# Two graph attention layers: the last attention's products issued as two column halves of the array

## The chip, the cores and the metric

The kernel runs on one core of a Trainium2 chip, in one launch. The metric is the device time of that core in microseconds (us); lower is better. Before the change the median of three runs is 3426.05 us, the lowest 3424.98 and the highest 3427.45.

A core has a matrix engine (TensorE), VectorE, ScalarE, GpSimd and DMA queues, here mostly issued from SyncE. TensorE computes `out = lhsT.T @ rhs`: the operand `lhsT` is loaded into the array first (an LDWEIGHTS record in the trace), then `rhs` streams past it (a MATMUL record) and the result is written to PSUM. The columns of `lhsT` become the partitions of the result.

## The reference

64 graphs of 256 nodes with 512 features each, all in fp32, go through two layers. Each layer normalises its input, applies a ReLU, runs attention over the edges of the graph and adds the result to its input. The second layer is the one that matters here. Cut to it:

```python
# x: (64, 256, 512), adj: (64, 256, 256); H = 8 heads of k = 64 features
h  = jnp.maximum(_layernorm(x, axis=-1), 0.0)
xp = jnp.einsum('bnd,do->bno', h, W_proj)
xh = xp.reshape(B, N, H, k).transpose(0, 2, 1, 3)
a_src = jnp.einsum('bhnk,hk->bhn', xh, W_att[:, :k])
a_dst = jnp.einsum('bhnk,hk->bhn', xh, W_att[:, k:])
scores = leaky_relu(a_src[:, :, :, None] + a_dst[:, :, None, :] + b_att[None, :, None, None], 0.2)
scores = jnp.where((adj > 0)[:, None, :, :], scores, -1e30)
att = softmax(scores, axis=-1)
out = relu(einsum('bhij,bhjk->bhik', att, xh))        # the products that are changed
x   = x + out.transpose(0, 2, 1, 3).reshape(B, N, H * k)
```

The first layer has two attentions of its own, with 4 heads of 256 features and with 1 head of 512 features.

## The kernel before

A graph passes through three attentions, numbered 1, 2 and 3. In each, VectorE and ScalarE build the unnormalised edge weights `e` of a head (256 x 256, source nodes on the partitions in two tiles `s`, target nodes along the row); TensorE multiplies them with the projected features `xl`, to which a column of ones is appended, so that the last column of the result is the sum of the weights; VectorE divides by it. The work of three successive graphs is interleaved by one hand-written order.

The large projections go through one helper, which holds most of TensorE's other work. Its products have 256 to 264 moving columns (`put` adds up partial sums of a Strassen-like scheme; seven such products stand for eight):

```python
P = 128                                                                # line 18
class Product:
    def product(self, to, i, first, last):
        for c in range(self.nk):
            self.nc.tensor.matmul(to[:, :self.n], self.lhs[:, i, c, :], self.rhs[:, i, c, :],      # line 54
                                  start=(first and c == 0), stop=(last and c == self.nk - 1),
                                  skip_group_check=True)
    def kept(self, name):
        s = self.work.tile([P, 268], F32, name=name)
        self.nc.scalar.activation(s[:, :self.n], self.sum[:, :self.n], AF.Copy)                    # line 60
        return s
    # ... p1 to p7: the products in their order ...
```

Buffers in PSUM, and the transposes and edge weights:

```python
T, G, K3, H3, Q = 2, 4, 64, 8, 256
ps_sum = tile_pool(name="ps_sum", bufs=2, space=PSUM)
ps_mm  = tile_pool(name="ps_mm", bufs=4, space=PSUM)
ps_tr  = tile_pool(name="ps_tr", bufs=2, space=PSUM)
xl3 = const.tile([P, T, H3, K3 + 1], F32, name="xl3")      # the last column is 1.0
# ...
nc.tensor.transpose(pt[:, k, t * P:(t + 1) * P], h(t, c + k), ident)                               # line 193
# ...
def weigh(dst, bc, xw, yw, mask, op):
    wy = work.tile([P, T, P], F32, name="wy", bufs=3)
    nc.scalar.activation(wy, bc, AF.Copy, scale=yw)                                                # line 273
    nc.vector.scalar_tensor_tensor(dst, wy.rearrange("p t q -> p (t q)"), xw, mask, ALU.max, op)   # line 274
```

The third attention, whose product is changed:

```python
def edges3(self, h):
    e = self.e[3, h] = work.tile([P, T, N], F32, name="e", bufs=8)
    for s in range(T):
        weigh(e[:, s, :], self.bc3[h], self.ex3[:, 0, h, s:s + 1], self.ex3[:, 1, h, s:s + 1],
              self.cap[:, s, :], ALU.min)

def gat3(self, a, t):                     # a: four heads of the eight, t: 128 nodes of the 256
    pm = self.pm = ps_mm.tile([P, 512], F32, name="pm")
    pv = pm[:, :G * (K3 + 1)].rearrange("p (h k) -> p h k", h=G)
    for h in range(G):
        for s in range(T):
            nc.tensor.matmul(pv[:, h, :], self.e[3, a * G + h][:, s, t * P:(t + 1) * P],           # line 445
                             xl3[:, s, a * G + h, :], start=(s == 0), stop=(s == T - 1))

def out3(self, a, t):
    pv = self.pm[:, :G * (K3 + 1)].rearrange("p (h k) -> p h k", h=G)
    r = small.tile([P, G, 1], F32, name="r3")
    nc.vector.reciprocal(r, pv[:, :, K3:])                                                         # line 451
    o = work.tile([P, G, K3], F32, name="o", bufs=4)
    nc.vector.scalar_tensor_tensor(o, pv[:, :, :K3], 0.0, r.to_broadcast([P, G, K3]), ALU.max, ALU.mult)
    # ... GpSimd adds o to x2 (line 455) ...
```

The products of attentions 1 and 2 (`gat1`, line 348, and `gat2`, line 399) have the same form, with 256 or 257 moving columns. The order in which the items are issued, cut to the places of gat3; `0` is the current graph, `-1` and `-2` are the two before it:

```python
order = """
    -1 exp2, -2 edges3 0, 0 m1a p2, ... -2 edges3 5,
    -2 gat3 0 0, -2 out3 0 0, 0 m1b p6, -1 edges2, -2 edges3 6, 0 m1b p5, -2 gat3 0 1, -2 out3 0 1, -2 edges3 7,
    0 m1b p7, 0 m1b c22, -1 gat2 0, ... -1 gat2 1, ... 0 gat1 0 0, 0 out1 0 0, -2 gat3 1 0,
    -2 out3 1 0, 0 cap3, -1 stats3 1, 0 gat1 0 1, -1 norm3, 0 out1 0 1, -2 gat3 1 1, 0 elu1 0 0, -2 out3 1 1, -2 store,
    0 gat1 1 0, ...
"""
```

Right at the end a product with 2 weight columns and 1 moving column folds a check over all partitions (line 601):

```python
nc.tensor.matmul(pf[:2, 0, 0:1], top[:, 2:4], ones, start=True, stop=True)                         # line 601
```

Of the kernel before, what the change touches and what calls it, by code (L numbers as in the profile page):

```python
# [17 lines left out]
P = 128  # L18
# [79 lines left out]
def short_path(ctx, tc, flags, x, adj, w1, att_src1, att_dst1, b1, w2, att_src2, att_dst2, b2, w_proj, w_att,  # L98
               b_att, out):

    nc = tc.nc
# [6 lines left out]
    T = N // P  # L108
    DC = D // P
    HC = HF // P  # L110
    G = 4
# [43 lines left out]
    xl3 = const.tile([P, T, H3, K3 + 1], F32, name="xl3")  # L155
# [120 lines left out]
    class Graph:  # L276
# [163 lines left out]
        def gat3(self, a, t):  # L440
            pm = self.pm = ps_mm.tile([P, 512], F32, name="pm")
            pv = pm[:, :G * (K3 + 1)].rearrange("p (h k) -> p h k", h=G)
            for h in range(G):
                for s in range(T):
                    nc.tensor.matmul(pv[:, h, :], self.e[3, a * G + h][:, s, t * P:(t + 1) * P],  # L445
                                     xl3[:, s, a * G + h, :], start=(s == 0), stop=(s == T - 1))

        def out3(self, a, t):
            pv = self.pm[:, :G * (K3 + 1)].rearrange("p (h k) -> p h k", h=G)
# [7 lines left out]
        def range(self):  # L457
            nc.vector.tensor_reduce(ends[:, 0, self.b:self.b + 1], self.exs, AX.X, ALU.max)
            nc.vector.tensor_reduce(ends[:, 1, self.b:self.b + 1], self.exs, AX.X, ALU.min)
# [408 lines left out]
```

## Time and profile before

The profiled execution spans 3421.9 us.

| engine | busy us | share of the span | instructions |
|---|---|---|---|
| TensorE, products (PE) | 3326.7 | 97% | 17668 |
| TensorE, weight loads (PEld) | 2899.3 | 85% | 17668 |
| VectorE (DVE) | 2492.3 | 73% | 6447 |
| ScalarE (ACT) | 1876.7 | 55% | 4481 |
| GpSimd (POOL) | 1231.4 | 36% | 1369 |

The page numbers its parts: busy times; the span in 40 slices, with busy tenths of each engine and the clock granted to TensorE; DMA queues; the chain of work that ended last, as shares of the span by engine and by line; and the costliest groups of instructions, with count, busy time, mean length in ns, and the idle time ahead of them with what ended it. "L445" is line 445 of the kernel. In the groups and in the timeline `out<-in` are the program's tiles; PEld is a weight load and PE a product. Products are pipelined, so that one record overlaps with the next: what one really costs is the step from one start to the next, not its length.

### The profile page before, as it was taken

Reading aid. Unit: us, or ns where it says so; the run is one execution under the profiler, and the core shown is the slowest. Engines: PE = TensorE matmul, PEld = TensorE weight load, DVE = VectorE, ACT = ScalarE, POOL = GpSimd, SP = SyncE. Lnnn points to the kernel's source line nnn. Section 1 sums busy time; section 2 is a strip of 40 time slices with the busy share of each in tenths; the row PEclk is TensorE's granted clock in tenths of the full one; section 3 lists DMA queues with packets and bytes.
Section 4 is the critical chain, followed back from the end, with each engine's and each line's share of the span. In section 5 each row is a group of like instructions: output and inputs, shape, how many; then the busy total and the mean of one; then the engine's idle time right before and its main releaser. Section 6 shows DMA issues by size and latency. Waiting matters only on the chain.

```text
span 3421.9 us, 51905 instructions
## 1 busy us (share of the span) xinstructions
PE 3326.7 (97%) x17668; PEld 2899.3 (85%) x17668; DVE 2492.3 (73%) x6447; ACT 1876.7 (55%) x4481; POOL 1231.4 (36%) x1369
## 2 busy tenths in 40 slices
PE   4899999999999999999999999999999999999997
PEld 3688888888888888888888888888888888888886
DVE  7577777777777777777777777777777777777773
ACT  2355555555555555555565565565565565555553
POOL 1333433333433433433433433433433434334332
PEclk8999999999999999999999999999999999999997
DMA  4223323323223233323323323323223233232331
GB/s 134 58 85 82 82 85 81 83 82 85 83 80 86 81 81 83 85 78 81 90 75 82 92 75 82 90 76 83 86 80 83 81 86 81 80 87 78 84 78 40
DMA packets 354316, 280.87 MB, mean 82 GB/s; under 512 B 159616, under 2 KB 254848, under 8 KB 354048
## 3 DMA queue, kind: packets, MB, share of 16 engines
q1 hardware_dynamic: 352480, 275.40, 29.7%
q8 instruction: 144, 2.36, 0.3%
q10 hardware_dynamic: 1568, 2.10, 0.2%
q14 instruction: 124, 1.02, 0.1%
HBM read 201.07 MB, written 67.96 MB: 79 GB/s over the span
## 4 chain that ended last, share of the span: by engine, by line
PE 88%; ACT 5%; DMA 3%; DVE 2%; issue 1%; POOL 0%; SPq 0%; ACTq 0%; DVEq 0%
PE sum L54 30%; PE pm L54 21%; PE pm L445 13%; PE pm L348 13%; PE pm L399 6%; PE pt L193 5%; ACT wy L273 3%; DMA kept<-exs 1%; DMA bc<-kept 1%; ACT u L60 1%; ACT s L60 0%; DVE wy L492 0%; DMA w1a_sb<-in_L_gnn_W_dram 0%; DVE e L274 0%; POOL o L553 0%
## 5 line engine op out<-in xcount | busy, mean ns | idle before, releaser
L273 ACT ACTIVATE wy<-bc,exs 128x256 f32<-128x256 f32 x1664 | 768.9, 520 | 194.5 <-DMA bc<-kept 79.2
L455 POOL TENSOR_TENSOR x<-x,o 128x256 f32<-128x256 f32 x256 | 197.7, 772 | 1446.0 <-DVE o L453 1446.0
L274 DVE SCALAR_TENSOR_TENSOR e<-wy,exs,cap 128x256 f32<-128x256 f32 x1024 | 486.4, 511 | 141.0 <-ACT wy L273 133.3
L445 PEld LDWEIGHTS pm<-xl,e 128*128 128x128 f32 x4096 | 505.4, 195 | 26.5 <-issue 9.8
L348 PE MATMUL pm<-xl,e 128*128 128x257 f32 x2048 | 496.6, 385 | 9.9 <-DVE e L274 6.5
L445 PE MATMUL pm<-xl,e 128*128 128x65 f32 x4096 | 494.5, 275 | 11.3 <-DVE e L274 11.3
L54 PE MATMUL sum<-w_sb,h1s 128*128 128x257 f32 x2048 | 493.7, 383 | 0.7 <-ACT u L60 0.7
L54 PEld LDWEIGHTS sum<-w_sb,h1s 128*128 128x128 f32 x2048 | 379.9, 190 | 73.6 <-issue 21.8
L246 DVE TENSOR_TENSOR xl<-pm,u 128x256 f32<-128x256 f32 (+2 forms) x512 | 214.8, 419 | 310.0 <-PE pm L54 249.8
L348 PEld LDWEIGHTS pm<-xl,e 128*128 128x128 f32 x2048 | 375.2, 191 | 59.2 <-DVE e L274 8.4
L60 ACT ACTIVATE u<-sum 128x260 f32<-128x260 f32 (+3 forms) x512 | 196.5, 384 | 356.7 <-PE sum L54 350.7
L54 PE MATMUL pm<-w_sb,h1s 128*128 128x257 f32 x1536 | 365.0, 379 | 0.0
L54 PEld LDWEIGHTS pm<-w_sb,h1s 128*128 128x128 f32 x1536 | 290.9, 189 | 43.9
L54 PE MATMUL sum<-w1a_sb,hs 128*128 128x260 f32 x1024 | 274.7, 391 | 36.0 <-DVE hs L206 28.8
L274 DVE SCALAR_TENSOR_TENSOR e<-wy,exs,mask 128x256 f32<-128x256 f32 x640 | 274.7, 476 | 46.9 <-ACT wy L273 46.9
L212 POOL TENSOR_TENSOR hs<-hs 128x256 f32<-128x256 f32 x128 | 93.6, 731 | 543.1 <-DVE hs L206 324.6
L54 PE MATMUL sum<-wp_sb,hs 128*128 128x264 f32 x1024 | 277.3, 393 | 1.2 <-ACT u L60 1.1
L54 PE MATMUL sum<-w1b_sb,hs 128*128 128x256 f32 x1024 | 271.1, 387 | 1.0 <-ACT u L60 1.0
L54 PEld LDWEIGHTS sum<-w1a_sb,hs 128*128 128x128 f32 x1024 | 188.4, 190 | 89.2 <-ACT u L60 32.1
L358 DVE SCALAR_TENSOR_TENSOR z<-pm,r,b_sb 128x256 f32<-128x256 f32 x512 | 247.7, 484 | 18.1
L361 ACT ACTIVATE ez<-z 128x512 f32<-128x512 f32 x256 | 160.4, 627 | 164.9 <-DVE z L358 164.7
L399 PE MATMUL pm<-xl,e 128*128 128x257 f32 (+1 forms) x1024 | 243.8, 381 | 0.8 <-DVE e L274 0.7
(92 smaller groups left out, 5284.7 us busy)
## 6 DMA issues: line engine op xcount, KB each, us to landing
bc<-kept SPq DMA_DIRECT2D x384, 256.0 KB, 3.8
xs<-in_x_dram SPq DMA_DIRECT2D x64, 512.0 KB, 3.9
kept_h<-h SPq DMA_DIRECT2D x64, 512.0 KB, 3.2
h<-kept_h SPq DMA_DIRECT2D x64, 512.0 KB, 3.6
out_dram<-x SPq DMA_DIRECT2D x64, 512.0 KB, 2.8
ad<-in_adj_dram SPq DMA_DIRECT2D x64, 256.0 KB, 4.2
bc<-kept SPq DMA_DIRECT2D x64, 128.0 KB, 4.2
w_sb<-in_L_gnn_W_dram SPq DMA_DIRECT2D x4, 512.0 KB, 9.2
```

The source lines that it names most:

```text
L54: self.nc.tensor.matmul(to[:, :self.n], self.lhs[:, i, c, :], self.rhs[:, i, c, :], start=(first and c == 0), stop=(last and c == self.nk ...
L60: self.nc.scalar.activation(s[:, :self.n], self.sum[:, :self.n], AF.Copy)
L193: nc.tensor.transpose(pt[:, k, t * P:(t + 1) * P], h(t, c + k), ident)
L246: nc.vector.tensor_tensor(dst, pm, add, ALU.add)
L273: nc.scalar.activation(wy, bc, AF.Copy, scale=yw)
L274: nc.vector.scalar_tensor_tensor(dst, wy.rearrange("p t q -> p (t q)"), xw, mask, ALU.max, op)
L348: nc.tensor.matmul(pm[:, :Q + 1], self.e[1, h][:, s, t * P:(t + 1) * P], xl1[:, s, h, L1:], start=(s == 0), stop=(s == T - 1))
L358: nc.vector.scalar_tensor_tensor(z[:, sl], pm[:, :Q], r, b1_sb[:, sl], ALU.mult, ALU.add)
L361: nc.scalar.activation(ez, z[:, 2 * g * F1:2 * (g + 1) * F1], AF.Relu, scale=-1.0)
L399: nc.tensor.matmul(pm[:, :n], self.e[2][:, s, t * P:(t + 1) * P], xl2[:, s, half, L2:L2 + n], start=(s == 0), stop=(s == T - 1))
L445: nc.tensor.matmul(pv[:, h, :], self.e[3, a * G + h][:, s, t * P:(t + 1) * P], xl3[:, s, a * G + h, :], start=(s == 0), stop=(s == T - 1))
L455: nc.gpsimd.tensor_tensor(to, to, o.rearrange("p h k -> p (h k)"), ALU.add)
```

## The change

`gat3` multiplies 128 x 128 edge weights with 128 x 65 features. The change issues each such product as two: the first takes the edge weights of 64 target nodes and writes the upper 64 partitions of the result, the second takes the other 64 nodes and writes the lower 64 partitions. Each has 64 weight columns and lies on its own half of the array's columns. The values computed, the tiles and the order are the same. It is meant to let the two halves of the array, each with its own weights, work at the same time, since a product with 65 moving columns keeps the array occupied with weight loads more than with streaming.

```diff
@@ -440,10 +440,12 @@
         def gat3(self, a, t):
             pm = self.pm = ps_mm.tile([P, 512], F32, name="pm")
             pv = pm[:, :G * (K3 + 1)].rearrange("p (h k) -> p h k", h=G)
+
             for h in range(G):
                 for s in range(T):
-                    nc.tensor.matmul(pv[:, h, :], self.e[3, a * G + h][:, s, t * P:(t + 1) * P],
-                                     xl3[:, s, a * G + h, :], start=(s == 0), stop=(s == T - 1))
+                    for q in range(0, P, 64):
+                        nc.tensor.matmul(pv[q:q + 64, h, :], self.e[3, a * G + h][:, s, t * P + q:t * P + q + 64],
+                                         xl3[:, s, a * G + h, :], start=(s == 0), stop=(s == T - 1))
```

## Prediction

> **What bounds the kernel now.** I read the busy times first, then the 40 slices, then the chain of work that ended last:
>
> ```profile
> PE 3326.7 (97%) x17668; PEld 2899.3 (85%) x17668; DVE 2492.3 (73%) x6447; ACT 1876.7 (55%) x4481; POOL 1231.4 (36%) x1369
> ...
> PE   4899999999999999999999999999999999999997
> ...
> PEclk8999999999999999999999999999999999999997
> ...
> PE 88%; ACT 5%; DMA 3%; DVE 2%; issue 1%; POOL 0%; SPq 0%; ACTq 0%; DVEq 0%
> PE sum L54 30%; PE pm L54 21%; PE pm L445 13%; PE pm L348 13%; PE pm L399 6%; PE pt L193 5%; ACT wy L273 3%; DMA kept<-exs 1%; DMA bc<-kept 1%; ACT u L60 1%; ACT s L60 0%; DVE wy L492 0%; DMA w1a_sb<-in_L_gnn_W_dram 0%; DVE e L274 0%; POOL
> ```
>
> TensorE is the bound from the third slice to the last, at full clock, with VectorE next at 73%. The line that the change touches, L445, holds 13% of the chain: 0.13 x 3422 = 445 us. Whatever it gains or loses goes almost straight into the time. The table of busy time by stretch, over three graphs' worth of the middle (1480 to 1636 us), shows how little slack TensorE has and how much the others have:
>
> ```profile
> 1480.00:1636.00 156.00, 155.65 (x839) 136.10 (x838) 115.50 (x296) 89.09 (x214) 58.41 (x65) 1.00 0.31 82
> ```
>
> (columns: length, PE, PEld, DVE, ACT, POOL, clock, DMA share, GB/s.) A graph costs 52 us, of which TensorE is idle 0.1 us.
>
> A busy TensorE may stream or load weights, so I took L445 apart. In the groups it stands twice, as loads and as products; in the timeline I looked at one call of gat3, weight loads first and then products:
>
> ```profile
> L445 PEld LDWEIGHTS pm<-xl,e 128*128 128x128 f32 x4096 | 505.4, 195 | 26.5 <-issue 9.8
> L445 PE MATMUL pm<-xl,e 128*128 128x65 f32 x4096 | 494.5, 275 | 11.3 <-DVE e L274 11.3
> ```
>
> ```profile
> 1506.88 0.19 PEld L54 LDWEIGHTS pm<-w1a_sb,hs 128*128 128x128 f32 x1
> 1507.10 1.97 PEld L445 LDWEIGHTS pm<-xl,e 128*128 128x128 f32 x16
> ```
>
> ```profile
> 1507.32 1.90 PE L445 MATMUL pm<-xl,e 128*128 128x65 f32 x16
> 1509.05 0.43 PE L54 MATMUL sum<-w1b_sb,hs 128*128 128x256 f32 x1
> ```
>
> The program asks for 64 graphs x 4 calls x 4 heads x 2 = 2048 products, and the trace has 4096 of each kind: every fp32 product is two records. Sixteen records take 1.97 us from the first load. The first load lies 0.22 us early, under the product before it, and the last is 0.19 long, so the 14 steps between take (1.97 - 0.22 - 0.19) / 14 = **0.111 us each**. What fills the 0.111? A line's own answer gives shortest, median and longest record:
>
> ```profile
> L445 PEld LDWEIGHTS pm<-xl,e x4096: 186/192/333, 165.9 to 3412.3; 128*128 128x128 f32 x196
> L445 PE MATMUL pm<-xl,e x4096: 220/275/444, 166.1 to 3412.4; 128*128 128x65 f32 x196
> ```
>
> ```profile
> L601 PEld LDWEIGHTS pt<-ones,top x2: 80/82/83, 3414.7 to 3414.7; 128*2 128x2 f32 x2
> L601 PE MATMUL pt<-ones,top x2: 163/164/165, 3414.7 to 3414.7; 128*2 128x1 f32 x2
> ```
>
> L601 is a tiny product near the end, with 2 weight columns and 1 moving column. Against it a load of 128 columns lasts 192 - 82 = 110 ns longer, 0.87 ns a column: a fixed 80 ns that overlaps with the neighbours, and 110 ns that don't. A product of 65 columns lasts at its shortest 220 - 164 = 56 ns longer than one of 1. So one step of 111 ns is **one weight load**; the streaming, 56 ns, lies under the next load. The usual product of 275 ns is the short one plus 55 ns in which it waits for its weights. On L54, with 256 to 264 moving columns, it is the other way round: loads hide under streaming.
>
> **What the Trainium skill says.** "TensorE: Matmul & The Clock Gate", section "LDWEIGHTS (loading the stationary operand)", has the load's time grow with the number of columns alone, columns / 1.2 ns. That is 107 ns for 128 columns; this trace agrees with 111 per step, and L601 confirms the growth. "FP8 and Floating Point Precision", section "TensorE Precision Notes", says that true FP32 is four passes through the array; two records a product, each 56 ns for 65 columns, fit that. "TensorEngine Tiling (Array Packing)", section "Key Properties", bears on the change itself: tiles of the array may load weights and multiply in parallel, but changing the tiling mode drains TensorE. The first page's "Measured speedup vs the span model" reports 2.38x for three column tiles with 512 moving columns, which shows products side by side, not loads. No run here has column tiles yet, so neither statement is seen in this trace.
>
> **The change part by part.** L445's 4096 records of 128 weight columns become 8192 of 64 columns each; the moving operand, 65 columns, is read once for each half. VectorE's, ScalarE's and GpSimd's work, the transfers and the PSUM tile stay as they are.
>
> (a) One load: 64 of 128 columns, 110 / 2 = 55 ns, say 58 with the step's small fixed part; in the trace its record should last 82 + 62 x 0.87 = 136 ns. The streaming stays 56 ns and still fits under a load of its size.
>
> (b) Two halves in place of one record. If the two tiles' loads run at once, an old step of 111 ns becomes 58, 53 ns less; over 4096 steps that is -217 us. Issue doesn't forbid it: L601's two products start 26 ns apart, each with its load, and 58 ns has to hold two such pairs. If all loads share one way in, 2 x 58 = 116, 5 more than now: 4096 x 5 = +20 us.
>
> (c) Mode changes. Each of the 256 calls stands alone between products of 128 columns (L54, L348, L399), so it is entered and left once, 512 changes. What one costs I estimate from the records: a product lasts 164 ns beyond its streaming (L601), and behind a drain the next weights, now loaded ahead, would follow only after that, with some 50 ns more until the first result streams. I take 0.2 us a change, 0.4 a call: 256 x 0.4 = +102 us.
>
> (d) Passing it on. In the stretch shown, 0.35 us of 156 are waits of TensorE, and VectorE has 115.5 of 156. A gain of (217 - 102) / 64 = 1.8 us a graph leaves VectorE far from being the bound. But when gat3 gets shorter, some products behind it (those waiting for a copy on L60 or for edge weights on L274) come earlier than their input: I take a tenth off. (217 - 102) x 0.9 = 104 us, 3426 - 104 = **3322, say 3320 us**.
>
> **Rivals.**
> 1. *Loads side by side, no drain to speak of.* -217 x 0.9 = -195: about 3230. For it: the page states that tiles work independently. Against it: the same page states the drain.
> 2. *Loads one after another.* In the call shown two loads of 128 columns never come closer than 0.11 us, so today one load is taken in at a time; if it stays so, +20 from (b) and from 0 to +102 from (c): 3445 to 3550. Here the change only moves the wait from one long load to two short ones.
> 3. *Nothing overlaps within a tile.* If a load of 64 columns can't be taken ahead of the running product of the same column tile, and the tiles also take turns, each half costs 58 + 56 = 114 ns and a step 228: 4096 x 117 = +479 us, about 3900. Against it: in the present mode loads do overlap with products on the same rows and columns. For it: no trace here shows what fp32 makes of the column mode. Overlap in part (tiles side by side, load and product of one tile in turn) gives 114 a step, like rival 2.
> 4. *VectorE or ScalarE becomes the bound.* Even rival 1 takes 3.1 of 52 us per graph, against VectorE's 38.5: it doesn't happen as a sum, at most as single waits.
>
> **Range and chances.** Loads side by side get 52% (30% with a drain near my estimate, 3310 to 3345; 22% with little of it, about 3230 to 3260). Loads in turn get 27%, half near 3445, half up to 3550. The rest, 21%, is the lack of overlap of rival 3, anywhere from 3550 to 3900. So low is 3225 and high 3560, with most of the miss above. Faster by over 2% (under 3357.5) 0.50, within 2% 0.18, slower (over 3494.6) 0.32.
>
> **What would show it.** In the profile after: L445 with 8192 loads of 128x64 at about 136 ns median, right for (a). In the timeline of one call, 32 loads within about 0.95 us for side by side, 1.85 us for in turn, 3.6 for rival 3. Around a call, the start of the first product after L54 and the start of the first L54 product after the call: 0.2 us later than 0.22 and 0.11 us for the drain, or not. The slices must keep PE at 9, the clock at 9; the waits of "PE sum" on "ACT u L60", 4.6 us now, growing to tens of us would show that step (d) was too small. The prediction is wrong if loads of the two tiles don't overlap, or if a change of mode costs more than 0.4 us, at which point the gain of a call (16 x 53 ns = 0.85 us) is used up.

## The result and the profile after

The median is 3385.75 us (3385.23 to 3385.99) against 3425.52 us of the kernel before on the same chip: ratio **0.988**, 95% interval 0.987 to 0.990, 40 us less. The prediction was 3320 us, 106 us less. The direction was right; the gain is 0.38 of the one forecast.

First the busy times of the page after, then the table of busy time by stretch over three graphs in the middle (length, PE, PEld, DVE, ACT, POOL, clock, DMA share, GB/s):

```profile
PE 3230.2 (95%) x21764; PEld 2659.8 (79%) x21764; DVE 2503.5 (74%) x6447; ACT 1868.1 (55%) x4481; POOL 1245.1 (37%) x1369
```

```profile
1480.00:1632.00 152.00, 149.05 (x1017) 122.98 (x1016) 114.29 (x291) 87.67 (x210) 57.87 (x63) 1.00 0.30 82
```

TensorE no longer fills the stretch: 2.95 us of 152 are idle, where 0.35 of 156 were before. That is 1 us a graph which the array had saved and then stood still for. (The chain that ended last breaks off after 1% of the span in this page, so it isn't read.)

Now the changed line, L447 after the edit. Its shortest, median and longest record:

```profile
L447 PEld LDWEIGHTS pm<-xl,e x8192: 132/138/232, 167.0 to 3373.5; 128*64 128x64 f32 x200
L447 PE MATMUL pm<-xl,e x8192: 220/222/370, 167.0 to 3373.6; 128*64 128x65 f32 x200
```

A load of 64 columns lasts 138 ns, against 192 for 128. A product's median is 222, the same as its shortest, against 275: it no longer waits 55 ns for its weights. In the timeline, one call of gat3 between two calls of gat1 (start, length, engine, line, tiles, shapes, records, and in brackets idle time with its releaser), before:

```profile
1519.76 0.81 PE L348 MATMUL pm<-xl,e 128*128 128x257 f32 x3
1520.41 1.90 PE L445 MATMUL pm<-xl,e 128*128 128x65 f32 x16
1522.14 1.95 PE L348 MATMUL pm<-xl,e 128*128 128x257 f32 x8
```

and after:

```profile
1506.23 1.03 PE L348 MATMUL pm<-xl,e 128*128 128x257 f32 x4
1507.21 1.15 PE L447 MATMUL pm<-xl,e 128*64 128x65 f32 x32
1508.30 1.13 PE L348 MATMUL pm<-xl,e 128*128 128x257 f32 x4
1509.78 0.46 PE L348 MATMUL pm<-xl,e 128*128 128x257 f32 x1 [0.35 <-DVE r L356]
```

From the call's first start to the next line's first it took 1522.14 - 1520.41 = 1.73 us; now 1508.30 - 1507.21 = 1.09 us, with twice the records. But gat1, which ran its 8 records in one go, now stops after four: its fifth waits until VectorE's reciprocal on L356 has given back a buffer of `pm`. The waits of the whole span show two pairs of entries, each for weight loads and for products, that the kernel before doesn't have at this size (total us, times, longest; a load and its product wait at the same time, so the two don't add up):

```profile
PEld pt L193 <- ACT h L186: 56.8, 128, 2.9
...
PEld pm L348 <- PE pm L348: 46.2, 64, 1.0
...
PE pt L193 <- ACT h L186: 28.3, 66, 2.7
PE pm L348 <- DVE r L356: 24.8, 64, 2.5
```

Before, the transposes on L193 waited 4.9 and 3.9 us for h (L186), and the two entries on `pm` stood at 1.3 and 3.4 us. Each of these waits comes once or twice for each of the 64 graphs.

The change of mode (from the whole array to two column halves, and back) shows at both ends of a call. Before, the first load of a call started 0.22 us ahead of its product, under the product before it (1507.10 and 1507.32 in the lines of the prediction). Now the loads of the same call of gat3, and those of gat1 behind it, start only with their products (1507.21 and 1508.30):

```profile
1507.19 1.03 PEld L447 LDWEIGHTS pm<-xl,e 128*64 128x64 f32 x32 [0.33 <-PE pm L348]
1508.29 0.73 PEld L348 LDWEIGHTS pm<-xl,e 128*128 128x128 f32 x4
```

To see where a graph loses what, I set the starts of all TensorE records of both traces side by side, in program order, over 50 graphs (mean, ns a graph; only rows that differ by over 40; a group is four records on L54):

```
stretch                                            before  after  difference
4 calls of gat3, first start to next line's start  4x1732  4x1083    -2596
first product group behind a call of a = 0 (2x)      918    968       +98
last group ahead of a call, entering the mode (2x)   870    963      +186
gat1 0 0, ahead of the third call                   1733   1861      +127
gat1 0 1, between the two calls of a = 1            1788   2522      +734
gat1 1 0, behind the fourth call                    1789   1854       +65
transposes of turn3                                  873   1525      +652
gat1 1 1, then the first product of m3              1879   2031      +152
```

These rows sum to -582; with the small ones a graph takes 0.56 us less, 64 x 0.56 = 36 us of the 40. Counting a call from entering the mode to having left it, for the a = 0 calls, which meet no wait: 649 - 93 - 49 = 507 ns, **0.507 us gained a call**, 2.03 us a graph, 130 us in all. About 1.4 us a graph of this, 70%, comes back as waits behind gat1 and ahead of turn3 and m3.

What is in that stretch? Busy time from the first edge weights of the first attention to the end of turn3's transposes, before and then after:

```profile
1516.99:1528.32 11.33, 11.33 (x73) 10.41 (x72) 10.66 (x35) 6.46 (x12) 2.36 (x4) 1.00 0.31 82
```

```profile
1504.50:1515.28 10.78, 10.05 (x102) 7.76 (x100) 10.39 (x34) 6.13 (x12) 2.38 (x4) 1.00 0.28 87
```

VectorE, 73% busy over the span, is busy for 10.66 of 11.33 us here, already before the change, and for 10.39 of 10.78 after. If it limits the stretch, TensorE can't cross it faster than VectorE works through its row: edge weights, division, statistics, division again. That is the theory that the experiments test. For h, a chain follows behind VectorE's part: its last step ends at 1511.86, then GpSimd needs until 1512.88, and only then does ScalarE write h, in two operations:

```profile
1511.70 0.16 DVE L176 TENSOR_SCALAR ve<-mv 128x2 f32<-128x2 f32 x1
1512.88 1.52 ACT L186 ACTIVATE h<-x,off,rstd 128x512 f32<-128x512 f32 x2 [1.33 <-POOL off L180]
```

### The profile page after: what moved, and what is told of

The parts are those of the page before. It is cut to its first block, busy times and chain, and to the rows that moved or that the text cites. A ratio compares the mean times of both kernels' runs of the same rounds, so it can differ in the third digit from the quotient of the medians.

```text
span 3383.4 us, 60097 instructions
## 1 busy us (share of the span) xinstructions
PE 3230.2 (95%) x21764; PEld 2659.8 (79%) x21764; DVE 2503.5 (74%) x6447; ACT 1868.1 (55%) x4481; POOL 1245.1 (37%) x1369
## 5 line engine op out<-in xcount | busy, mean ns | idle before, releaser
L348 PE MATMUL pm<-xl,e 128*128 128x257 f32 x2048 | 518.8, 391 | 32.0 <-DVE r L356 24.8
L54 PE MATMUL sum<-w_sb,h1s 128*128 128x257 f32 x2048 | 493.8, 383 | 0.7 <-ACT u L60 0.7
L348 PEld LDWEIGHTS pm<-xl,e 128*128 128x128 f32 x2048 | 362.6, 190 | 118.0 <-PE pm L348 46.2
L54 PEld LDWEIGHTS sum<-w_sb,h1s 128*128 128x128 f32 x2048 | 379.9, 190 | 73.7 <-issue 21.9
L54 PE MATMUL pm<-w_sb,h1s 128*128 128x257 f32 x1536 | 365.3, 379 | 0.0
L60 ACT ACTIVATE u<-sum 128x260 f32<-128x260 f32 (+3 forms) x512 | 195.4, 382 | 287.0 <-PE sum L54 281.4
L447 PEld LDWEIGHTS pm<-xl,e 128*64 128x64 f32 x8192 | 265.9, 139 | 99.1 <-issue 52.2
L54 PEld LDWEIGHTS pm<-w_sb,h1s 128*128 128x128 f32 x1536 | 291.2, 190 | 44.0
L212 POOL TENSOR_TENSOR hs<-hs 128x256 f32<-128x256 f32 x128 | 127.0, 992 | 518.0 <-DVE hs L206 330.6
L274 DVE SCALAR_TENSOR_TENSOR e<-wy,exs,mask 128x256 f32<-128x256 f32 x640 | 303.7, 524 | 17.2 <-ACT wy L273 9.9
L447 PE MATMUL pm<-xl,e 128*64 128x65 f32 x8192 | 302.1, 227 | 12.9 <-DVE e L274 12.6
L54 PE MATMUL sum<-w1a_sb,hs 128*128 128x260 f32 x1024 | 274.7, 391 | 36.1 <-DMA e<-in_L_gnn_att_src_dram 28.9
L54 PE MATMUL sum<-wp_sb,hs 128*128 128x264 f32 x1024 | 277.3, 393 | 9.3 <-ACT u L60 1.1
L54 PE MATMUL sum<-w1b_sb,hs 128*128 128x256 f32 x1024 | 277.4, 393 | 1.0 <-ACT u L60 1.0
L54 PEld LDWEIGHTS sum<-w1a_sb,hs 128*128 128x128 f32 x1024 | 188.4, 190 | 89.4 <-ACT u L60 31.8
L367 DVE SCALAR_TENSOR_TENSOR z<-ez,z 128x512 f32<-128x512 f32 x256 | 206.7, 808 | 64.0 <-ACT ez L362 64.0
```

The source lines that it names most:

```text
L212: nc.gpsimd.tensor_tensor(s1, s3, a22, ALU.add)
L348: nc.tensor.matmul(pm[:, :Q + 1], self.e[1, h][:, s, t * P:(t + 1) * P], xl1[:, s, h, L1:], start=(s == 0), stop=(s == T - 1))
L367: nc.vector.scalar_tensor_tensor(z, self.e["ez", g, t], -1.0, z, ALU.add, ALU.max)
L447: nc.tensor.matmul(pv[q:q + 64, h, :], self.e[3, a * G + h][:, s, t * P + q:t * P + q + 64], xl3[:, s, a * G + h, :], start=(s == 0), stop ...
```

## The experiments

Ratios are to the kernel before, run on the same chip at the same time, with 95% intervals. "A graph" is the median distance, over 47 graphs, between the first gat2 records of one graph and the next, worked out from the trace of each run. It is 51.57 us before and 50.98 after the change.

| run | what | ratio | a graph, us |
|---|---|---|---|
| the change | all calls in halves | 0.988 (0.987 to 0.990) | 50.98 |
| e1 | halves in the a = 0 calls alone | 0.991 (0.989 to 0.993) | 51.07 |
| e2 | halves in the a = 1 calls alone | 0.992 (0.991 to 0.994) | 51.17 |
| e3 | second half left out | a single run | 50.78 |
| e4 | four quarters | 0.989 (0.987 to 0.991) | 51.11 |
| e5 | halves, new order | 0.963 (0.961 to 0.965) | 49.62 |
| e6 | whole, new order | 0.994 (0.992 to 0.995) | 51.29 |
| e7 | halves, less VectorE work | 0.974 (0.972 to 0.975) | 50.20 |
| e8 | as e5, gat1 in halves too | 0.964 (0.962 to 0.966) | 49.56 |
| e9 | as e5, calls in pairs | 0.963 (0.962 to 0.964) | 49.62 |
| e10 | as e6, calls in pairs | 1.002 (1.001 to 1.003) | 51.74 |

### e1 and e2: one part of the change alone

```diff
-                    for q in range(0, P, 64):
+                    n = 64 if a == 0 else P          # e2: a == 1
+                    for q in range(0, P, n):
```

> Only the calls for the first four heads (a = 0) are split, 128 of 256; the others stay whole. Theory 'slack': each split call shortens TensorE's way by 0.51 us after its mode changes are paid, so two a graph give 1.01 us; between the second attention's last product and the last transposes of the third layer's input TensorE has about 1.2 us of slack against VectorE's row of work, which two calls fit into and four do not. Then 64 x 1.01 = 65 us off the kernel before, about 3361, faster than with all four split. Rival 'a=1 calls lose': only the calls that stand inside that stretch lose, the same 3361 here, but a loss in the sister run. Rival 'VectorE limits the whole graph': half of the change's gain of 40 us, about 3406.

> Only the calls for the last four heads (a = 1) are split. Theory 'slack': the gain of 1.01 us a graph just about fits into the slack, with up to 0.2 us lost: 50 to 65 us off, 3360 to 3376. Rival 'a=1 calls lose': in the trace of the change the sum over these two calls and the waits behind them is +0.45 us a graph, so 29 us more than before, about 3454. Rival 'VectorE limits the whole graph': about 3406.

Measured: 0.991 and 0.992. Two calls keep 0.51 (e1) and 0.40 us (e2) of their 1.01 us a graph, four calls 0.60. So all three expectations fell in size. "The a = 1 calls lose" is out: e2 is faster than before, not slower. "VectorE limits the whole graph" (3406, a ratio of 0.994) lies outside the interval of e1 and just above that of e2; what puts it out for good is e5, which does the same work in less time. The slack that I took, 1.2 us ahead of turn3, was too large: I had looked at one wait only. The first product of m3 has none. It needs ScalarE's copies of the transposes (L226), and it already waited for them before the change (24.5 us over the span, 34.0 after it):

```profile
PEld sum L54 <- ACT hs L226: 24.5, 64, 0.5
```

In e1 and e2 as well as in the change, the stretch from gat1 1 1 to m3 takes 0.15 us more than before.

### e3: do the two tiles work at the same time?

Only the first 64 of each 128 nodes get this attention's result; division and addition are cut to the same 64 partitions.

```diff
-                    for q in range(0, P, 64):
+                    for q in range(0, 64, 64):
```

> Leaves out the second half: only the products of the first 64 of each 128 target nodes are issued, and their results alone are divided and added; the other nodes lack this attention. Per call 16 records in one column tile in place of 32 in two. Theory 'tiles side by side': a record of one tile costs 58 ns, load-bound, whether the other tile works or not, so the 16 starts of a call stretch over 0.9 us as the 32 do (0.93). Rival 'loads are just faster in this mode, and in turn': a record costs 29 ns, and the call's starts stretch over 0.45 us.

One call in e3's timeline, TensorE's products:

```profile
1506.61 1.13 PE L447 MATMUL pm<-xl,e 128*64 128x65 f32 x16
```

16 records take as long (1.13 us, first start to last end) as the 32 of the change (1.15). From the median of 248 calls, the starts stretch over 0.92 us in place of 0.93. So the second tile costs nothing: the tiles load and stream side by side. The first step of a call is 107 ns long in both runs, and every later one 58 ns: for one record in e3, for a pair in the change. "In turn, but faster" would have given 0.45 us and is out.

### e4: four tiles

```diff
-                    for q in range(0, P, 64):
-                        nc.tensor.matmul(pv[q:q + 64, h, :], ...[:, s, t * P + q:t * P + q + 64],
+                    for q in range(0, P, 32):
+                        nc.tensor.matmul(pv[q:q + 32, h, :], ...[:, s, t * P + q:t * P + q + 32],
```

> Four quarters of 32 nodes each in place of two halves of 64, 64 records a call. Theory 'tiles side by side, streaming 56 ns next': a load of 32 columns takes some 29 ns, but 65 moving columns still take 56, so a step of four stays near 58 ns if nothing else limits, and the time is that of the change, 3386. Rival 'issue': products have not started closer than 25 ns on average in any trace, so four cost at least 100 ns, a call 1.6 us or more, all of the gain is gone and with the mode changes the time is 3426 to 3470.

```profile
1501.54 1.11 PE L447 MATMUL pm<-xl,e 128*32 128x65 f32 x64
```

64 records in the 1.11 us that 32 took. The issue rival fell: records start 0.896 / 63 = 14 ns apart on average. Nothing more is won either, although a load's record is shorter still (109 ns against 138): four records take 57 ns together where two take 58. The streaming of some 56 ns, which doesn't shrink with the weight columns, fits that step; no run changes it, so this cause is argued and not shown. 0.989 is not told apart from the change's 0.988.

### e5 and e6: another order in the stretch, with halves and with whole products

```diff
-        -1 gat2 1, 0 edges1 1, -1 out2 1, 0 edges1 2, 0 edges1 3, 1 load, 0 gat1 0 0, 0 out1 0 0, -2 gat3 1 0,
-        -2 out3 1 0, 0 cap3, -1 stats3 1, 0 gat1 0 1, -1 norm3, 0 out1 0 1, -2 gat3 1 1, 0 elu1 0 0, -2 out3 1 1, -2 store,
-        0 gat1 1 0, 0 out1 1 0, -1 turn3, 0 elu1 0 1, 0 gat1 1 1, 0 out1 1 1, 0 elu1 1 0, 0 elu1 1 1,
+        -1 gat2 1, 0 edges1 1, -1 out2 1, -1 stats3 1, 1 load, 0 gat1 0 0, 0 out1 0 0, 0 edges1 2, -2 gat3 1 0,
+        -2 out3 1 0, 0 cap3, -1 norm3, 0 gat1 0 1, 0 out1 0 1, 0 edges1 3, 0 ez1 0 0, -2 gat3 1 1, -2 out3 1 1, -2 store,
+        -1 turn3, 0 ez1 0 1, 0 elu1 0 0, 0 gat1 1 0, 0 out1 1 0, 0 elu1 0 1, 0 gat1 1 1, 0 ez1 1 0, 0 out1 1 1,
+        0 elu1 1 0, 0 ez1 1 1, 0 elu1 1 1,
```

`ez1` holds the Relu and the Exp that stood at the end of `out1`. The work is the same; what TensorE needs soonest now stands first in VectorE's and ScalarE's rows.

> The change (all calls in halves) with another order of issue in one stretch: edges1 2 behind out1 0 0 and edges1 3 behind out1 0 1, stats3 1 right behind out2 1, norm3 and turn3 earlier, and the two Exp operations of out1 in items of their own. Nothing else differs and all is computed. Theory 'VectorE's row of work in this stretch': the waits that the change brought (0.73 us for a buffer of pm behind out1 0 0, 0.65 us for h ahead of turn3, 0.15 us ahead of m3 p1, a graph) go away in large part: 1.0 to 1.5 us a graph, 64 to 96 us less than the change, 0.960 to 0.970 of the kernel before. Rival 'limit elsewhere' (VectorE or a transfer over the whole graph, or the mode changes): TensorE waits elsewhere instead and the ratio stays at 0.985 to 0.99.

> The same order of issue with whole products, as a control. Theory 'VectorE's row of work': the kernel before has 0.1 us of waits a graph in the middle, so a better order has nothing to give: ratio 0.997 to 1.003. Rival 'the order is better by itself': as much gain here as in the run with halves, 0.97 to 0.98.

e5 over three graphs:

```profile
1480.00:1629.00 149.00, 148.61 (x1023) 124.44 (x1022) 113.94 (x296) 87.08 (x212) 58.10 (x63) 1.00 0.33 86
```

TensorE is idle for 0.39 us of 149 again, and the ratio is 0.963, inside what the theory expected. The waits that the change had brought are gone: that on `pm` (L356, 24.8 us after the change) no longer stands in the list, and that for h, 28.3 us after the change, has shrunk to 3.7:

```profile
PE pt L193 <- ACT h L186: 3.7, 4, 1.6
```

The control e6 gives 0.994, a little more than the 0.997 I had set as its limit: 0.28 us a graph. Its trace shows where: gat1 1 0 and 1 1 now follow each other behind turn3 and take 3.47 us in place of 1.79 + 1.88, and the first group of m3 takes 0.89 in place of 0.99, because turn3's copies are ready in time. So the order gives 0.6% by itself and 2.6% with halves. Put the other way: with the old order halves are worth 40 us, with the new one 0.963 / 0.994 = 0.969 or **about 106 us**, and 51.29 - 49.62 = 1.67 us of the 2.03 a graph are kept.

### e7: less work in VectorE's row

```diff
         def edges1(self, h):
+            if h == 3:
+                self.e[1, 3] = self.e[1, 2]
+                return
```

> The change in its own order, but head 3 of the first attention takes head 2's edge weights in place of its own: leaves out two of ScalarE's and two of VectorE's operations a graph in the stretch (0.42 us each on VectorE, 0.85 in all) and no product. Theory 'VectorE's row of work': the buffers and h come 0.85 us earlier, the waits shrink by about that: 45 to 60 us less than the change, ratio 0.970 to 0.976. Rival 'limit elsewhere': less than 15 us, ratio 0.984 or more.

Measured 0.974, and 50.98 - 50.20 = 0.77 us a graph less than the change, of the 0.85 us of VectorE work that was left out. TensorE's own work is the same. Of the products' waits (24.8 us on `pm` and 28.3 for h after the change), the first is gone, and the second is smaller although TensorE now comes to it 0.59 us earlier:

```profile
PE pm L351 <- DVE r L359: 2.7, 1, 2.7
PE pt L193 <- ACT h L186: 19.7, 64, 2.7
```

This shows that the stretch is set outside TensorE. It takes away ScalarE's share of the edge weights too, so it doesn't tell VectorE from ScalarE; for VectorE speaks the busy time of the stretch, 10.39 of 10.78 us against ScalarE's 6.13. Nor does it say how much of the wait for h is the chain over GpSimd and ScalarE. More buffers for `pm` were not tried.

### e8: longer streams in halves

```diff
+                n = 64 if g == 0 else P
                 for s in range(T):
-                    nc.tensor.matmul(pm[:, :Q + 1], self.e[1, h][:, s, t * P:(t + 1) * P], xl1[:, s, h, L1:],
+                    for q in range(0, P, n):
+                        nc.tensor.matmul(pm[q:q + n, :Q + 1], self.e[1, h][:, s, t * P + q:t * P + q + n],
```

> The new order with halves, and gat1's products of the first two heads (257 moving columns) in halves as well, so that four calls in a row stay in one mode: three of the eight mode changes of a graph and part of a fourth go away. A mode change costs about 0.12 us beyond what it hides. Theory 'tiles side by side' for long streams too: gat1's calls stay as long as they are, 0.3 to 0.4 us a graph less than the new order alone, 20 to 26 us, ratio about 0.007 lower. Rival 'two streams of 257 columns share something': gat1's two calls get longer, up to twice 1.73 us, and the time grows by up to 220 us.

0.964, not told apart from e5. Streams of 257 columns run side by side too: the first of these gat1 calls takes 1.78 us from its first start to gat3's (median of 62), against 1.85 in e5, where that contains a mode change, and 1.73 before, without one. But the second still takes 2.13 against 2.15, and the loads' wait for edge weights has grown from 15.4 us in e5 to 39.3:

```profile
PEld pm L350 <- DVE e L274: 39.3, 90, 5.7
```

The expectation of 20 to 26 us failed. It had counted too many mode changes: in this order four stays in the mode (a stay is what lies between entering and leaving it) become three, which saves two changes of eight. And what was saved came back further on. Set beside e5 (medians), a graph is 0.17 us shorter from gat2 1 to the last of the four calls, and 0.17 us longer in the second attention's projection, where a product waits for ScalarE's copy on L60.

### e9 and e10: fewer mode changes

```diff
-        -2 gat3 0 0, -2 out3 0 0, 0 m1b p6, -1 edges2, -2 edges3 6, 0 m1b p5, -2 gat3 0 1, -2 out3 0 1, -2 edges3 7,
+        -2 gat3 0 0, -2 out3 0 0, -2 gat3 0 1, -2 out3 0 1, 0 m1b p6, -1 edges2, -2 edges3 6, 0 m1b p5, -2 edges3 7,
...
-        0 edges1 2, -2 gat3 1 0, -2 out3 1 0, 0 cap3, -1 norm3, 0 gat1 0 1, 0 out1 0 1, 0 edges1 3, ...
+        0 edges1 2, 0 gat1 0 1, 0 cap3, -1 norm3, 0 out1 0 1, -2 gat3 1 0, -2 out3 1 0, 0 edges1 3, ...
```

> The new order with halves, and besides the two calls of the same four heads one right behind the other on TensorE, so that a graph has two stays in the mode of halves in place of four. Theory 'a mode change costs': from the trace of the change a call keeps 0.51 us of the 0.83 us that its 16 steps save, so entering and leaving cost 0.32 us; two fewer of these a graph are 0.64 us, 41 us, if no new wait comes, and half of it if VectorE's row takes some: ratio 0.951 to 0.957 after 0.963. Rival 'the changes are free, the rest of the call was waiting': no difference, 0.963, or more if the pair waits for edge weights.

> The same order with pairs and whole products, as a control. Theory 'a mode change costs': there is none here, so the order of pairs gives what the new order gave, 0.994, give or take 0.002. Rival 'pairs are the better order by themselves': another 0.006 to 0.012 less here too.

In the timeline of e9 two calls are one stay of 64 records:

```profile
1509.09 0.82 PE L54 MATMUL pm<-w1a_sb,hs 128*128 128x260 f32 x3
1509.84 2.09 PE L449 MATMUL pm<-xl,e 128*64 128x65 f32 x64
1511.86 0.91 PE L54 MATMUL sum<-w1b_sb,hs 128*128 128x256 f32 x3
```

From the start of the record ahead to the start of the record behind, a pair of a = 0 takes 2.33 us where two single calls of the change take 1.39 each. One stay contains 0.22 us of the record ahead, so the pair spares 2 x 1.39 - 2.33 - 0.22 = 0.24 us; with the 0.10 us that the first group behind a stay takes longer than other groups (0.97 against 0.86), about 0.35, near the 0.32 expected. With whole products the same sum gives nothing: in e10 the pair takes 3.74 us from record to record, against 2 x 1.95 - 0.22 = 3.68, which costs 0.05, and 0.05 is spared in the group behind. So a **stay costs about 0.35 us**.

The time is still 0.963, as in e5. Set beside e5 (medians), a graph of e9 is 0.62 us shorter around its two pairs and 0.67 us longer elsewhere: 0.30 at the same place as in e8, 0.15 in the last two calls of gat1, 0.12 in two groups of m3, and 0.10 in gat2. The place of the 0.30 in e9's timeline:

```profile
1495.14 0.68 ACT L432 ACTIVATE exs<-lg 128x16 f32<-128x16 f32 x3 [3.13 <-DVE lg L246]
1496.23 1.98 PE L54 MATMUL sum<-w_sb,h1s 128*128 128x257 f32 x8 [0.34 <-ACT u L60]
```

ScalarE stands for 3.13 us until VectorE brings the input of an exponential (exp3), and the copy that TensorE needs (L60) comes behind it in ScalarE's row. The control e10 shows that the order of pairs has a price by itself: with whole products it costs 51.74 - 51.29 = 0.45 us a graph against e6 (1.002 after 0.994), though at other places, 0.39 of it around the pair of a = 1. The cost of a mode change is shown by the length of the stay; a gain in the total needs an order that doesn't cost it back, and none was found.

## Why the prediction was wrong in size

- **What bounds the kernel: right for the span, not for every stretch.** TensorE was the bound, and a step of L445 was one weight load: with half the columns a load lasts 138 ns (136 foretold), and the products stopped waiting for it.
- **(a) and (b): right.** Loads of the two tiles run side by side (e3). Behind the first pair of records, one in each half, a pair takes 58 ns, as foretold, where a whole record took 112. A second call right behind a first adds 0.93 us in halves (e9) and 1.79 with whole products (e10): 0.85 us less, the 0.85 of the prediction.
- **(c): right in kind, somewhat too large.** 0.852 - 0.507 = 0.345 us a stay, 0.40 foretold. What the array gained, 256 x 0.507 = 130 us, was therefore even above the 115 of the prediction.
- **(d), "I take a tenth off": this is the step that failed.** It was worth 70% in place of 10%. The prediction compared VectorE's 115.5 us with 156 over three graphs and called it far from the bound; over the 11 us in which gat1, two calls of gat3 and turn3 lie it was busy for 94% already before. There TensorE waited for VectorE's row, and for the chain behind it over GpSimd and ScalarE, as soon as it got faster. The waits that the prediction named as the sign of this error ("PE sum" on "ACT u L60", 4.6 us before) stayed at 4.2, and grew only in the new order with pairs, to 23.1 in e9; they came on `pm` behind L356 and on h (L186) instead.
- **The rivals.** 1 had the loads right and fell on the 0.35 us a stay that it took for nothing. 2 and 3 are out by the 58 ns a pair, and e3 shows that this is no faster load in turn. 4 was dismissed "as a sum", and its own words, "at most as single waits", are what happened: single waits of 0.7 us, 64 times each. The measured 3386 us lies between the ranges of the prediction's branches (up to 3345 for loads side by side, from 3445 for loads in turn): no branch foretold it.
- With the stretch reordered (e5 against e6) halves bring about 106 us, close to the 104 of the sum. That is partly luck: the 130 us were above the 115 of the sum, and 18% of them were lost in place of a tenth. The array's part of the sum was sound; how much of it TensorE could pass on was not.

## What to carry to other kernels

Before you credit a saving on the busiest engine, find the stretch in which it falls and take the other engines' busy time there, not over a period: an engine at 73% over the span can be at 94% where it counts, and then the saving becomes a wait for its buffers and results. When a faster part is nearly worthless, try the order of issue with and without it: here the two together gave 3.7%, the sum of each alone 1.8%. Products with few moving columns that are bound by weight loads can be worth splitting over column tiles, if a stay holds enough of them: here 16 records gained 0.85 us and a stay cost about 0.35.

## What the hardware showed that I had not expected

- The second column tile was free for these fp32 products: 16 records in one tile stretch over 0.92 us, 32 in two over 0.93, 64 in four over 0.90 (e3, the change, e4). In four tiles products start 14 ns apart on average.
- Two tiles streaming 257 columns at once took hardly longer than the same products at full width: 1.78 us for a call of gat1 (e8) against 1.73 (before).
- A stay in column tiles cost about 0.35 us: 0.09 us ahead of its first record, 0.05 in the group behind it, and 0.2 within, where the second pair starts 0.11 us after the first in place of 0.06, and the next line's first record 0.15 us after the last one. At both ends the first weights were no longer loaded ahead.
